# Layer 1 of a two-layer convolution and attention model: normalization as one factor a token, sent to all partitions by DMA

## The chip, the cores and the metric

The kernel runs on one core of a Trainium2 chip. A core has four engines that compute: TensorE (PE in the profile) multiplies matrices, with weight loads shown apart (PEld); VectorE (DVE), ScalarE (ACT) and GpSimd (POOL) work on elements. SyncE (SP) starts DMA transfers, one after the other, in the order of its own instructions. TensorE writes to PSUM, which has eight banks of 128 partitions by 512 fp32 values; DVE and ACT read it from there[...]. The metric is the time of one execution on the device in microseconds. Everything is fp32, but for two masks.

## The reference

The input x has the shape (4, 128, 64, 64). Layer 0 is a convolution and a local attention in windows of 16 by 16. Layer 1 takes each of the 4 x 4096 pixels as a token of 128 channels, and it normalizes every token twice: ahead of a linear causal attention, and ahead of a recurrent network.

```python
def _ln_t(v, eps=1e-5):
    m = jnp.mean(v, axis=-1, keepdims=True)
    s = jnp.var(v, axis=-1, keepdims=True)
    return (v - m) / jnp.sqrt(s + eps)

def _L1_attn_ref(x, W, b):
    qkv = (x @ W.T + b).reshape(Bx, Tx, 3, Dx)
    q, k, v = (qkv[:, :, 0], qkv[:, :, 1], qkv[:, :, 2])
    q = jax.nn.elu(q) + 1.0
    k = jax.nn.elu(k) + 1.0
    # num = q . cumsum(k v^T), den = q . cumsum(k)
    return num / den

def _L1_ffn_ref(x, W, V, gamma, beta):
    Wx = jnp.einsum('bti,hi->bth', x, W)
    # Wx normalized over all tokens (mean and variance of each channel), then
    # the recurrence yt = sigmoid(wx_t + yt @ V.T) over the tokens
    ...

x = _L0_conv_ref(x, ...)              # layer 0
t = _to_tokens(x)                     # layer 1
t = t + _L1_attn_ref(_ln_t(t), L1_attn_W, L1_attn_b)
t = t + _L1_ffn_ref(_ln_t(t), L1_ffn_W, L1_ffn_V, L1_ffn_gamma, L1_ffn_beta)
```

## The kernel before

The image is worked on in 16 bands of 16 rows (1024 tokens), each with four windows of layer 0. While TensorE goes through the windows of one band, layer 1 of the band before it is worked on in between: it is cut into small steps, and after each part of a window (six gaps a window) one step of layer 1 and one of the next band's convolution are put in. `in_order` then fixes that order on TensorE, DVE, ACT and GpSimd. SP's own order is left to the scheduler. A band of layer 1 has two halves of 512 tokens, `a` and `c`; `y` and `z` are the two halves of the band before, whose last steps are still due.

```python
p1, p2, p3 = ...   # pools with 1, 2 and 3 buffers a tag; bank() is one of 8 PSUM banks

def measured(pieces, eps):              # mean and 1/sqrt(var + eps) of each token
    for j, piece in enumerate(pieces):
        nc.vector.bn_stats(st[:, j, :], piece)                                # L191
    for j in range(n):
        nc.vector.bn_aggr(mv[:, j, :], st[:, j, :])                           # L193
    nc.gpsimd.tensor_scalar(rs[:, :n], mv[:, :n, 1], eps, 1.0, ALU.add, ALU.mult)  # L195
    nc.gpsimd.tensor_tensor(rs[:, :n], rs[:, :n], mhalf[:, :n], ALU.pow)      # L196
    return pieces, mv, rs

def normed(found, tiles, tag):          # tokens lie on partitions here
    for j, piece in enumerate(pieces):
        nc.vector.tensor_scalar(                                              # L203
            xn[:, j, :], piece, mv[:, j, 0:1], rs[:, j : j + 1], ALU.subtract, ALU.mult
        )
    return xn

def turned(xn, j0, n):                  # channels to partitions, through TensorE
    tps = bank()
    for j in range(n):
        nc.tensor.transpose(tps[:, j * P : (j + 1) * P], xn[:, j0 + j, :], ident)  # L212
    return tps

def taps(...): ...                      # convolution: eight multiply-adds of DVE, L288

def window_inputs(w, n, wj): ...        # q, k (L337), v (L350); two small DMAs for v (L359, L360)

def weighted(w):                        # layer 0: sums of the softmax, and its output
    ...                                 # sums on TensorE (L400)
    nc.scalar.copy(den, dps)                                                  # L403
    nc.sync.dma_start(dc, den[::HD, :])                                       # L405
    yield
    ...                                 # attention output on TensorE (L412)
    nc.scalar.copy(o_sb, ops)                                                 # L420
    yield
    nc.vector.tensor_tensor(dc, dc, pad_c, ALU.add)                           # L423
    nc.vector.reciprocal(rc, dc)                                              # L425
    nc.sync.dma_start(rd.rearrange("h (a e) -> (h a) e", e=16), rc)           # L429
    nc.sync.dma_start(rden, rd.unsqueeze(1).to_broadcast([HEADS, HD, BR * WT]))  # L431
    w["o"], w["rden"] = o_sb, rden

def scaled(n, wj, w):                   # output divided by the sums
    nc.gpsimd.tensor_tensor(oTs[n][...], w["o"]..., w["rden"]..., ALU.mult)   # L440

def output0(h):                         # layer 0's output, and x added
    ...
    nc.tensor.matmul(yps[:, j * P : (j + 1) * P], oT[:, br, t], woT[:, br, :], ...)  # L465
    nc.vector.tensor_tensor(h.x, yps..., xin[h.n][...], ALU.add)              # L472

def measure(h):
    h.found = measured([h.x[:, j, :] for j in range(4)], 1e-5)

def norm(h):
    h.xn = normed(h.found, p3, "xn")

def turn(h):
    h.xl = p2.tile([P, 512], F32, tag="xl", name="xl")
    nc.scalar.copy(h.xl, turned(h.xn, 0, 4))                                  # L489

def feature(h, m):                      # queries and keys: L494 on TensorE, L496 on ACT,
    ...                                 # L498 and L499 on DVE
def values(h): ...                      # L511 on TensorE, L519 on DVE
def scores(h): ...                      # L537 on TensorE, L539 on DVE
def attend(h, e): ...                   # L573, L575 on TensorE; L583 to L587 on DVE add to h.x

def keep(h):                            # x turned, for the very last addition
    rs = p1.tile([P, SEG, HSEGS], F32, tag="rs_o", name="rs_o")
    nc.scalar.copy(rs, turned(h.x, 0, 4).rearrange("p (k s) -> p s k", s=SEG))  # L592
    nc.sync.dma_start(resd[h.b][:, h.hb], rs.rearrange("p s k -> p (s k)"))   # L593

def turn_last(h):
    h.xl = p2.tile([P, 512], F32, tag="xl2", name="xl2")
    nc.scalar.copy(h.xl, turned(h.xn, 0, 4))                                  # L597

def product(h):                         # W x of the recurrent network, and its statistics
    wps = bank()
    nc.tensor.matmul(wps, fwT, h.xl, start=True, stop=True)                   # L602
    nc.scalar.copy(wx[:, h.b, h.hb], wps.rearrange("p (k s) -> p s k", s=SEG))  # L603
    nc.vector.bn_stats(stats[...], wx[...])                                   # L604
```

Behind the bands comes a short second phase: the kept x is loaded again from HBM (L748), and the recurrence runs in 128 segments side by side, eleven steps to warm up and then 32 (L771 to L823).

Of the kernel before, what the change touches and what calls it, by code (L numbers as in the profile page):

```python
# [9 lines left out]
F32 = mybir.dt.float32  # L10
# [36 lines left out]
def conv_attn_hybrid(ctx: ExitStack, tc: tile.TileContext, ins: dict, out: bass.AP):  # L47
# [10 lines left out]
    def loaded(name, shape, dt=F32, src=None, eng=None):  # L58
# [19 lines left out]
        pattern=[[1, P]],  # L78
        channel_multiplier=-1,
    )  # L80
    mhalf = const.tile([P, NCH], F32, name="mhalf")
    nc.vector.memset(mhalf, -0.5)

# [49 lines left out]
    def prepare():  # L133


        rect = math.sqrt(1.0 + LAM * LAM * (BR - 1))
        nc.vector.tensor_scalar(woT[:, 0], woT[:, 0], 1.0 / rect, None, ALU.mult)
        nc.vector.tensor_scalar(woT[:, 1], woT[:, 1], LAM / rect, None, ALU.mult)
        nc.vector.tensor_scalar(ab1, ab[:, :2], 1.0, None, ALU.add)


    dmax = const.tile([P, 16], F32, name="dmax")
# [33 lines left out]
    def bank():  # L176
        return ps.tile([P, 512], F32, tag="bank", name="bank")
# [21 lines left out]
    def normed(found, tiles, tag):  # L199
        pieces, mv, rs = found  # L200
        xn = tiles.tile([P, 4, P], F32, tag=tag, name=tag)
# [5 lines that stand above are left out]
# [272 lines left out]
            del oTs[h.n], xin[h.n]  # L479

    def measure(h):
        h.found = measured([h.x[:, j, :] for j in range(4)], 1e-5)

    def norm(h):
        h.xn = normed(h.found, p3, "xn")

    def turn(h):
        h.xl = p2.tile([P, 512], F32, tag="xl", name="xl")
        nc.scalar.copy(h.xl, turned(h.xn, 0, 4))  # L489

    def feature(h, m):

# [95 lines left out]

    def keep(h):

        rs = p1.tile([P, SEG, HSEGS], F32, tag="rs_o", name="rs_o")
        nc.scalar.copy(rs, turned(h.x, 0, 4).rearrange("p (k s) -> p s k", s=SEG))  # L592
        nc.sync.dma_start(resd[h.b][:, h.hb], rs.rearrange("p s k -> p (s k)"))  # L593

    def turn_last(h):
        h.xl = p2.tile([P, 512], F32, tag="xl2", name="xl2")
        nc.scalar.copy(h.xl, turned(h.xn, 0, 4))  # L597

    def product(h):

        wps = bank()
        nc.tensor.matmul(wps, fwT, h.xl, start=True, stop=True)  # L602
        nc.scalar.copy(wx[:, h.b, h.hb], wps.rearrange("p (k s) -> p s k", s=SEG))  # L603
        nc.vector.bn_stats(  # L604
            stats[:, h.b * NH + h.hb, :], wx[:, h.b, h.hb].rearrange("p s k -> p (s k)")
        )

    def layer1(n, last):
# [2 lines left out]
        y, z = last  # L611
        order = [
            (keep, z), None,
            (norm, z), (product, y), None,
            (output0, a), (measure, a), None,
            (turn_last, z), None,
            (norm, a), (output0, c), (measure, c), None,
            (turn, a), None,
            (product, z), (norm, c), None,
            (queries, a), None,  # L620
            (keys, a), None,
            (turn, c), None,
            (values, a), None,
            (queries, c), None,
            (scores, a), None,
# [5 lines left out]
            (attend, a, 0), None,  # L631
            (attend, a, 1), (measure, a), None,
            (scores, c), (keep, a), None,
            (accumulate, c), (norm, a), None,
            (attend, c, 0), None,
            (turn_last, a), (attend, c, 1), (measure, c), None,
        ]
        for what in order:
            if what is None:
# [5 lines left out]
    halves = {}  # L645

    def layer1_end(y, z):
        norm(z)
        product(y)
        yield  # L650
        keep(z)
        turn_last(z)
        yield
        product(z)

# [43 lines left out]
    for i in range(len(places) + 2):  # L699
# [5 lines left out]
        if 2 <= i:  # L705
            m, wjm = places[i - 2]
            if wjm == NB - 1:
                run(behind)
                behind = layer1(m, halves.pop(m - 1, (None, None)))
        between(i, 0)  # L710
        if 2 <= i:
            scaled(m, wjm, windows.pop(i - 2))
# [802 lines left out]
```

## Time and profile before

| | |
|---|---|
| time, median of 3 | 934.3 us (933.74 to 934.84) |
| span of the profiled run | 930.9 us |
| busy: PE, weight loads, DVE | 876.9, 656.1, 741.1 us |
| busy: ACT, POOL | 539.1, 262.4 us |
| granted TensorE clock | 0.975 |
| moved by DMA | 63.46 MB |

The page names each group of instructions by line, engine, operation and tiles. A timeline line has the start, the time taken, the engine, the line, the operation, and in brackets how long the engine had stood idle and what ended that. Several instructions of one line in a row are merged, with their count behind an x, and the time of such a group runs up to the end of its last one. Matmuls overlap, so what one of them costs is read from the next start, not from its own duration.

### The profile page before, as it was taken

Reading aid. Unit: us, or ns where it says so; the run is one execution under the profiler, and the core shown is the slowest. Engines: PE = TensorE matmul, PEld = TensorE weight load, DVE = VectorE, ACT = ScalarE, POOL = GpSimd, SP = SyncE. Lnnn points to the kernel's source line nnn. Section 1 sums busy time; section 2 is a strip of 40 time slices with the busy share of each in tenths; the row PEclk is TensorE's granted clock in tenths of the full one; section 3 lists DMA queues with packets and bytes.
Section 4 is the critical chain, followed back from the end, with each engine's and each line's share of the span. In section 5 each row is a group of like instructions: output and inputs, shape, how many; then the busy total and the mean of one; then the engine's idle time right before and its main releaser. Section 6 shows DMA issues by size and latency. Waiting matters only on the chain.

```text
span 930.9 us, 26534 instructions
## 1 busy us (share of the span) xinstructions
PE 876.9 (94%) x10508; PEld 656.1 (70%) x10508; DVE 741.1 (80%) x2452; ACT 539.1 (58%) x1010; POOL 262.4 (28%) x359
## 2 busy tenths in 40 slices
PE   4978999999999999999999999999999999987985
PEld 3756777877777777777787777787777777755442
DVE  6464978888897988797988888798878786676886
ACT  3755566565756565656656575656566665422552
POOL 2122131413232322313041323232232312121184
PEclk9988999999999999999999999999999999988897
DMA  4111121121222121212121121212121111102853
GB/s 121 34 44 56 47 72 37 54 57 57 59 63 59 49 57 50 69 49 73 37 56 57 52 59 60 62 48 62 48 66 48 49 37 60 43 24 73 345 205 129
DMA packets 53045, 63.46 MB, mean 68 GB/s; under 512 B 22960, under 2 KB 33840, under 8 KB 52400
## 3 DMA queue, kind: packets, MB, share of 16 engines
q1 hardware_dynamic: 51184, 56.91, 19.8%
q10 hardware_dynamic: 1728, 4.77, 1.3%
q8 instruction: 85, 1.39, 0.6%
q14 instruction: 48, 0.39, 0.1%
HBM read 35.44 MB, written 17.30 MB: 57 GB/s over the span
## 4 chain that ended last, share of the span: by engine, by line
PE 60%; DVE 26%; issue 4%; ACT 4%; DMA 3%; POOL 3%; ACTq 0%; SPq 0%; DVEq 0%; POOLq 0%
DVE y L288 8%; PE bank L337 8%; PE bank L465 6%; PE bank L382 6%; PE bank L212 6%; PE bank L494 5%; PE bank L400 4%; PE bank L350 4%; PE bank L412 4%; PE bank L602 3%; DVE st L191 2%; PE bank L815 2%; PE bank L537 2%; PE bank L573 2%; DVE state L562 2%
## 5 line engine op out<-in xcount | busy, mean ns | idle before, releaser
L288 DVE SCALAR_TENSOR_TENSOR y<-ypad,cpe_w,y 128x512 f32<-128x512 f32 x240 | 189.8, 791 | 15.1 <-ACT y L286 11.7
L391 ACT ACTIVATE es<-bank 128x512 f32<-128x512 f32 x256 | 132.2, 603 | 77.1 <-PE bank L382 77.1
L440 POOL TENSOR_TENSOR oT<-o_sb,rden 128x512 f32<-128x512 f32 x64 | 86.6, 1354 | 243.1 <-DMA rden<-rd 165.8
L195 POOL TENSOR_SCALAR rs<-mv 128x4 f32<-128x4 f32 (+2 forms) x100 | 25.1, 251 | 364.4 <-DVE mv L193 163.2
L203 DVE TENSOR_SCALAR xn<-x,mv,rs 128x128 f32<-128x128 f32 x256 | 90.8, 416 | 26.5 <-POOL rs L196 26.5
L196 POOL TENSOR_TENSOR rs<-rs,mhalf 128x4 f32<-128x4 f32 (+2 forms) x100 | 106.2, 1062 | 8.3
L382 PEld LDWEIGHTS bank<-q,k 32*128 32x128 f32 x3072 | 97.7, 189 | 7.8 <-ACT k L345 6.6
L382 PE MATMUL bank<-q,k 32*128 32x96 f32 (+1 forms) x3072 | 96.3, 270 | 1.1 <-ACT k L345 1.1
L412 PEld LDWEIGHTS bank<-es,v_sb 128*32 128x32 f32 x3072 | 56.8, 110 | 30.2 <-issue 18.6
L465 PE MATMUL bank<-woT,oT 128*128 128x128 f32 x512 | 68.1, 289 | 5.7 <-POOL oT L440 5.7
L465 PEld LDWEIGHTS bank<-woT,oT 128*128 128x128 f32 x512 | 64.8, 202 | 9.7 <-POOL oT L440 7.3
L412 PE MATMUL bank<-es,v_sb 128*32 128x96 f32 (+1 forms) x3072 | 70.1, 240 | 0.0
L494 PE MATMUL bank<-xl,awT 128*128 128x512 f32 x128 | 70.0, 630 | 0.0
L400 PE MATMUL bank<-es,ones 128*32 128x512 f32 x512 | 69.1, 612 | 0.0
L357 ACT COPY v_sb<-bank 128x512 f32<-128x512 f32 x64 | 37.5, 586 | 53.5 <-PE bank L350 42.2
L337 PE MATMUL bank<-y2w,wqT 128*128 128x256 f32 x256 | 66.4, 382 | 1.0 <-DVE y2w L288 1.0
L337 PE MATMUL bank<-y2w,wkT 128*128 128x256 f32 x256 | 65.8, 380 | 0.0
L350 PE MATMUL bank<-wvT,y2w 128*128 128x256 f32 x256 | 65.8, 380 | 0.0
L345 ACT COPY q<-bank 128x512 f32<-128x512 f32 x64 | 37.6, 587 | 41.3 <-PE bank L337 39.2
L345 ACT COPY k<-bank 128x512 f32<-128x512 f32 x64 | 37.3, 583 | 36.8 <-PE bank L337 36.7
L191 DVE BATCH_NORM_STATS2 st<-x 128x6 f32<-128x128 f32 x256 | 55.5, 280 | 1.1
L337 PEld LDWEIGHTS bank<-y2w,wqT 128*128 128x128 f32 x256 | 45.8, 194 | 12.8 <-issue 7.2
(124 smaller groups left out, 1728.4 us busy)
## 6 DMA issues: line engine op xcount, KB each, us to landing
rden<-rd SPq DMA_DIRECT2D x64, 256.0 KB
v_sb<-v_sb SPq DMA_DIRECT2D x128, 64.0 KB
resd<-rs_o SPq DMA_DIRECT2D x32, 256.0 KB
out<-ot SPq DMA_DIRECT2D x32, 256.0 KB
xin<-in_xt SPq DMA_DIRECT2D x15, 512.0 KB
res<-resd SPq DMA_DIRECT2D x2, 2048.0 KB
res<-resd ACTq DMA_DIRECT2D x2, 2048.0 KB
dc<-den SPq DMA_DIRECT2D x64, 8.0 KB
```

What stands on the lines that cost most here:

```text
L196: nc.gpsimd.tensor_tensor(rs[:, :n], rs[:, :n], mhalf[:, :n], ALU.pow)
L203: nc.vector.tensor_scalar(xn[:, j, :], piece, mv[:, j, 0:1], rs[:, j : j + 1], ALU.subtract, ALU.mult)
L288: nc.vector.scalar_tensor_tensor(y2, src, cpe_w[:, tap : tap + 1], y2, ALU.mult, ALU.add)
L337: nc.tensor.matmul(pps[:, br * WT : (br + 1) * WT], wT[:, br * P : (br + 1) * P], y2, start=True, stop=True,)
L350: nc.tensor.matmul(vps[:, e * 256 : (e + 1) * 256], y2[:, e * P : (e + 1) * P], wvT, start=True, stop=True,)
L382: nc.tensor.matmul(sps[h][:, cols], w["k"][rows, k0 : k0 + P], w["q"][rows, cols], start=False, stop=(br, n) == pieces[-1],)
L391: nc.scalar.activation(es, sps[h], AF.Exp, scale=scale)
L400: nc.tensor.matmul(dps[rows], ones[:, :HD], w["es", h], start=True, stop=True)
L412: nc.tensor.matmul(ops[rows, cols], w["v"][:, n, c0 : c0 + HD], w["es", h][:, cols], start=(br, n) == pieces[0], stop=(br, n) == pieces[-1],)
L440: nc.gpsimd.tensor_tensor(oTs[n][:, :, :, wj * WS : (wj + 1) * WS], w["o"].rearrange("p (a r c) -> p a r c", a=BR, c=WS), w["rden"].rearra ...
L465: nc.tensor.matmul(yps[:, j * P : (j + 1) * P], oT[:, br, t], woT[:, br, :], start=br == 0, stop=br == BR - 1,)
L494: nc.tensor.matmul(zps, awT[:, m * P : (m + 1) * P], h.xl, start=True, stop=True)
```

## The change

The normalization of layer 1 is (x - mean) times one factor a token. Both parts are taken out of the elementwise work on x. The mean is removed by the weights: with C = I - 1/128, W C x is W (x - mean), so awT and fwT are multiplied by C once. The factor rs stays as a multiplication of whole tokens, and it may come behind the transposes, or behind W, where tokens lie along the free axis. For that, rs is needed on all partitions: it is written to HBM (2 KB) and read back by every partition (256 KB). The second transposition of x, `turn_last`, goes away with its copy: `keep` has x turned already, and `product` now takes it from there. The order of the steps is changed so that the factor has some gaps to arrive in. What ACT copied out of PSUM in `turn` and `product` is now multiplied by DVE.

```diff
+    center = const.tile([P, P], F32, name="center")
+    nc.vector.tensor_scalar(center, ident, -1.0 / P, None, ALU.add)
...
+    def centre(w):
+        cps = bank()[:, : w.shape[1]]
+        nc.tensor.matmul(cps, center, w, start=True, stop=True)
+        nc.vector.tensor_copy(w, cps)
...
     def measure(h):
-        h.found = measured([h.x[:, j, :] for j in range(4)], 1e-5)
-
-    def norm(h):
-        h.xn = normed(h.found, p3, "xn")
+        _, _, rs = measured([h.x[:, j, :] for j in range(4)], 1e-5)
+        there = dram4.tile([P, 4], F32, tag="rs_d", name="rs_d")
+        nc.sync.dma_start(there, rs)
+        h.rs = p3.tile([P, 512], F32, tag="rs_b", name="rs_b")
+        nc.sync.dma_start(h.rs, there.rearrange("p j -> (p j)").partition_broadcast(P))

     def turn(h):
         h.xl = p2.tile([P, 512], F32, tag="xl", name="xl")
-        nc.scalar.copy(h.xl, turned(h.xn, 0, 4))
+        nc.vector.tensor_tensor(
+            h.xl.rearrange("p (j t) -> p j t", j=4),
+            turned(h.x, 0, 4).rearrange("p (j t) -> p j t", j=4),
+            h.rs.rearrange("p (t j) -> p j t", j=4),
+            ALU.mult,
+        )
...
     def keep(h):
-        rs = p1.tile([P, SEG, HSEGS], F32, tag="rs_o", name="rs_o")
-        nc.scalar.copy(rs, turned(h.x, 0, 4).rearrange("p (k s) -> p s k", s=SEG))
-        nc.sync.dma_start(resd[h.b][:, h.hb], rs.rearrange("p s k -> p (s k)"))
-
-    def turn_last(h):
-        h.xl = p2.tile([P, 512], F32, tag="xl2", name="xl2")
-        nc.scalar.copy(h.xl, turned(h.xn, 0, 4))
+        h.xs = p2.tile([P, SEG, HSEGS], F32, tag="rs_o", name="rs_o")
+        nc.scalar.copy(h.xs, turned(h.x, 0, 4).rearrange("p (k s) -> p s k", s=SEG))
+        nc.sync.dma_start(resd[h.b][:, h.hb], h.xs.rearrange("p s k -> p (s k)"))

     def product(h):
         wps = bank()
-        nc.tensor.matmul(wps, fwT, h.xl, start=True, stop=True)
-        nc.scalar.copy(wx[:, h.b, h.hb], wps.rearrange("p (k s) -> p s k", s=SEG))
+        nc.tensor.matmul(wps, fwT, h.xs.rearrange("p s k -> p (s k)"), start=True, stop=True)
+        n = P // SEG
+        nc.vector.tensor_tensor(
+            wx[:, h.b, h.hb].rearrange("p s (j n) -> p s j n", n=n),
+            wps.rearrange("p (s j n) -> p s j n", n=n, j=4),
+            h.rs.rearrange("p (n s j) -> p s j n", n=n, j=4),
+            ALU.mult,
+        )
...
         order = [
             (keep, z), None,
-            (norm, z), (product, y), None,
+            (product, y), None,
             (output0, a), (measure, a), None,
-            (turn_last, z), None,
-            (norm, a), (output0, c), (measure, c), None,
-            (turn, a), None,
-            (product, z), (norm, c), None,
-            (queries, a), None,
+            (output0, c), (measure, c), None,
+            None,
+            (product, z), None,
+            (turn, a), None,
+            None,
+            (queries, a), (turn, c), None,
             (keys, a), None,
-            (turn, c), None,
             (values, a), None,
...
             (attend, a, 1), (measure, a), None,
             (scores, c), (keep, a), None,
-            (accumulate, c), (norm, a), None,
+            (accumulate, c), None,
             (attend, c, 0), None,
-            (turn_last, a), (attend, c, 1), (measure, c), None,
+            (attend, c, 1), (measure, c), None,
...
     def layer1_end(y, z):
-        norm(z)
         product(y)
         yield
         keep(z)
-        turn_last(z)
         yield
         product(z)
...
+        if i == 2:
+            centre(awT)
+            centre(fwT)
```

## The prediction, made before the changed kernel ran

> **What bounds the kernel now.** I read the busy shares first, then the table by stage, the chain that ended last, TensorE's timeline over one band, and last the waits. The stage table (columns: stretch, its length, then busy us of PE, weight loads, DVE, ACT, POOL, each with its count, the granted clock, DMA share and GB/s) says that from 126 to 779 us TensorE is never short of work:
>
> ```profile
> 277.00:327.00 50.00, 49.57 (x649) 37.83 (x641) 42.48 (x142) 31.02 (x58) 14.01 (x19) 1.00 0.20 55
> 429.00:479.00 50.00, 49.76 (x629) 37.93 (x632) 43.00 (x143) 30.91 (x58) 14.19 (x19) 1.00 0.19 56
> 821.00:862.00 41.00, 31.78 (x168) 23.31 (x168) 29.14 (x102) 11.81 (x20) 5.76 (x13) 0.83 0.14 51
> ```
>
> In the middle TensorE has 49.6 of 50 us, DVE 42.5 and ACT 31; in the last band (821 to 862) nobody is full, so latency counts there. Matmul ends are modelled, so I checked on the timeline whether the starts really follow each other. They do, with few holes. Around the meeting of two bands:
>
> ```profile
> 420.93 1.01 PE L212 MATMUL bank<-ident,xn 128*128 128x128 f32 x4
> 421.77 0.39 PE L573 MATMUL bank<-v,aT 128*128 128x129 f32 x2
> ...
> 427.91 1.09 PE L412 MATMUL bank<-es,v_sb 128*32 128x96 f32 x48
> 428.93 2.05 PE L465 MATMUL bank<-woT,oT 128*128 128x128 f32 x16
> 430.82 1.03 PE L337 MATMUL bank<-y2w,wqT 128*128 128x256 f32 x4
> 431.69 0.60 PE L212 MATMUL bank<-ident,xn 128*128 128x128 f32 x4
> 432.12 1.03 PE L337 MATMUL bank<-y2w,wkT 128*128 128x256 f32 x4
> ```
>
> Four transposes at 431.69 push the next matmul back by 0.43 us: 0.109 each, that is their real price, not the 0.27 of the group's mean. The four at 420.93 took 0.84 until the next start, because each waited for one normalization on DVE. The same bands repeat at L465 starts of 378.39, 428.93, 479.39, 529.49: 50.4 us a band.
>
> What can hold L465 besides TensorE is oT, the product that GpSimd forms once rden, the softmax divisors, have come back by DMA. It is nearly as late as TensorE already:
>
> ```profile
> 417.96 0.19 POOL L195 TENSOR_SCALAR rs<-mv 128x4 f32<-128x4 f32 x1
> 418.24 1.01 POOL L196 TENSOR_TENSOR rs<-rs,mhalf 128x4 f32<-128x4 f32 x1
> ...
> 426.80 1.28 POOL L440 TENSOR_TENSOR oT<-o_sb,rden 128x512 f32<-128x512 f32 x1
> ```
> ```profile
> 417.17 0.32 SPq L593 DMA_DIRECT2D resd<-rs_o  x1
> 419.20 0.33 SPq L429 DMA_DIRECT2D rd<-rc  x1
> 420.66 0.58 SPq L431 DMA_DIRECT2D rden<-rd  x1
> ```
>
> oT ends at 428.08 and L465 starts at 428.93: slack 0.85 us. By the trace's record of landings rd takes 1.40 us and rden 5.34, so rden is there at 426.00, 0.80 before oT starts. In some bands (378.39, 580.22) L465 starts only when oT ends.
>
> **What the Trainium skill says.** (1) "DMA: Bandwidth & Descriptors", section "Why a DMA increments its semaphore by 16 and not by 1": a transfer is spread over as many engines as divide its outermost dimension. The trace agrees: rden (outermost 4, 256 KB) takes a median 5.25 us, resd (128 rows, 256 KB) 2.00. The new broadcast has 128 outermost, so I take 2.0 us for it when nothing is ahead. (2) "SBUF — State Buffer", section "SBUF: two separate sides": DVE and GpSimd exclude each other on a shared port for a whole instruction. The trace agrees: L203 mostly takes 0.34 us, but up to 1.31 beside GpSimd. Removing L203 removes these. (3) "SBUF — State Buffer", section "Door 1: The DMA port swizzle": each access that leaves a 16-byte line costs extra. The new multiply reads rs_b in steps of 16 bytes; no operation here shows the size of it.
>
> **The change part by part.** *Removed.* TensorE: 4 transposes for each of 32 halves (turn_last), 128 x 0.109 = 14.0 us, plus the waits for xn at 420.93, some 0.4 us a band. DVE: 256 normalizations, 90.8 us busy. ACT: the copies L489, L597 and L603, 19.0 + 18.8 + 20.1 = 57.9 us. *Added.* DVE: two multiplies a half from PSUM, 64 x 0.685 (as L519 and L472 of the same shape) = 43.8 us, perhaps 1.0 each with the strided operand. DMA: 64 writes of 2 KB and 64 broadcasts of 256 KB, 16.8 MB on top of 63.5, all in the one SP queue. Two centring matmuls once, with their copies to SBUF: about 0.5 us of it seen. DVE falls by 47 and ACT by 58 us; neither is the bound, so this is worth little by itself.
>
> If only TensorE counted, a band would lose 8 x 0.109 + 0.4 = 1.3 us, and 15 bands 19 us: 915. But the order of the instructions on SP says otherwise. In the last window of a band it becomes: write of rs, resd, rd, broadcast of rs, rden. In time of the old trace: rs leaves GpSimd at 419.25, its write is issued at 419.3, resd at 419.65 and rd at 420.0 instead of 419.20. Now resd stands right ahead of rd; where this happens already (812.4 and 812.8) rd took 1.79 instead of 1.40. It lands at 421.8, rden is issued at 421.9 instead of 420.66, and lands at about 427.4. oT then runs until 428.7 and L465 starts at 428.8, not 428.93, though TensorE would be there at 428.0. Of the gain ahead of L465 only 0.15 us is left. The transposes at 431.69 are behind L465, and their 0.44 is gained in full. So 0.6 us a band, 14 full bands: -8.4.
>
> *Turn and product.* From rs(a) ready (434.3) I count 1.5 for the write, then xin's 512 KB stands ahead (landing at 438.6 or so), then the broadcast: 439.3. DVE is ready for turn(a) at 438.4 and stands 0.9 us, while the queries' matmul comes at 441: hidden. For c the write waits behind rden's engines until about 442.6, and its broadcast lands at about 445; DVE stands 1.5 us for turn(c). Before, DVE idled 1.2 us at 452, and that is what pays for it: hidden, but only just.
>
> *Last band.* The late rden costs 1.8 us, less the 0.4 gained: +1.4. There the way from statistics to the first projection becomes 1.4 + 2.0 + 0.7 in place of normalization, transposes and copy (1.1 + 0.4 + 0.6): +2.0, of which shorter DVE queues give back 1.5. The end of layer 1 has the same trade and no large balance. +0.5.
>
> Sum: 934.3 - 8.4 + 1.4 + 0.5 + 0.5 = 928.3, put at 928.
>
> **The rivals.** *A, TensorE alone bounds it.* If rden comes as early as before (resd and rd not in each other's way), the 1.3 us a band are gained in full: 914 to 917. For it: PE is 60% of the chain, and DVE and ACT are relieved. Against it: 0.80 us of slack ahead of oT and at least 0.8 of added issue time in the same queue. *B, the broadcasts come late.* If turn(c)'s factor lands 1 us later than I count, or the strided multiply takes 1.1 us, DVE goes late into its full stretch (403 to 420 in the trace has no idle time), rc and rden slip with it, and each band pays 0.6 to 1.5 us: 937 to 950. For it: transfers issued behind xin and rden in this trace take 4.5 to 5.9 us instead of 1.9. Against it: the features of a, the next thing on DVE, come ahead of turn(c). *C, nothing to be seen.* oT takes up all of it, 932 to 935.
>
> **Range and chances.** My own account gives 928, A the lower edge (914), B beyond the upper (943). A at its best barely reaches the 2% line (915.6), so faster by over 2% gets 0.12. Slower by over 2% needs more than 953, B at its worst and in every band: 0.08. The rest, 0.80, lies within.
>
> **What would show it.** Right, if in the changed profile the bands repeat every 49.6 to 50.0 us, L465 waits for oT in most bands (the list of waits gives 5 of its matmuls and 5 of its weight loads now, 13.0 us in all; then 20 or more), rden is issued 1.0 to 1.5 us later after the attention sums than before, and DVE waits about 1 us for rs_b in each turn. Wrong towards A, if L465 has no more waits for oT and bands take 49.1. Wrong towards B, if TensorE waits for xl ahead of the queries, or the multiply has a mean above 1 us. Wrong altogether, if the last band and the recurrence behind it move by more than 4 us.

## The result, and the profile after

The changed kernel takes 1046.6 us (median of four runs) against 934.6 for the kernel before beside it: 1.120 times as long, with a 95% interval of 1.116 to 1.124. The prediction was 928, within 914 to 943. It is wrong by 119 us.

Where do they lie? In the two profiled runs (1044.3 and 930.9 us) I take the start of output0's first matmul in each band (L474 now, L465 before) as a mark. From the first band's mark to the last band's it is 839.3 us now and was 745.1: +94. From the last mark to the first matmul of the warm-up behind layer 1 (L822 now, L803 before) it is 63.0 and was 41.2: +22. Everything else is 2.6 us shorter. The middle bands repeat every 56.5 us instead of 50.3.

First the table by stage of the changed kernel, one band and the end of layer 1, with the columns of the prediction:

```profile
529.00:585.00 56.00, 50.56 (x636) 39.09 (x637) 41.42 (x129) 27.91 (x50) 13.28 (x19) 0.97 0.28 69
915.00:978.00 63.00, 29.10 (x156) 22.31 (x156) 28.53 (x87) 7.24 (x12) 5.81 (x13) 0.69 0.45 163
```

TensorE is busy 50.6 of 56 us, so it no longer sets the pitch, and the granted clock has left 1.00. The timeline where two bands meet shows what happens there (line numbers have moved by 9: L449 is oT, L474 output0, L346 q):

```profile
526.97 0.59 ACT L429 COPY o_sb<-bank 128x512 f32<-128x512 f32 x1
527.73 1.26 POOL L449 TENSOR_TENSOR oT<-o_sb,rden 128x512 f32<-128x512 f32 x1 [3.03 <-DMA rden<-rd]
...
529.04 2.64 PE L474 MATMUL bank<-woT,oT 128*128 128x128 f32 x16 [2.19 <-POOL oT L449]
...
531.48 1.91 PE L346 MATMUL bank<-y2w,wqT 128*128 128x256 f32 x4
```

TensorE stands for 2.19 us, because oT stands for rden. The matmul L346, which took 1.03 us at the same place before, then takes 1.91. The table by stage, cut at the change of the clock, says why (only the granted clock, the third number from the right, matters here):

```profile
529.00:530.30 1.30, 1.26 (x11) 1.26 (x12) 0.00 (x0) 0.00 (x0) 0.00 (x0) 1.00 0.38 107
530.30:533.70 3.40, 3.40 (x15) 3.04 (x14) 1.91 (x11) 0.27 (x1) 0.01 (x1) 0.50 0.35 116
```

A pause of 2.2 us is followed here by 3.4 us at half the clock, which costs 1.7 us more. Before, the clock records show half clock for 0.8 us between the first and last marks, the first 15 us left out; now for 64.0 us.

Not every such pause is followed by half clock. In this trace the half-clock records begin and end on one grid of 3.41 us, and what counts is how much of one interval of this grid TensorE stands. The pause shown lies with 2.13 us inside the interval from 526.92 to 530.33, and the next interval is at half clock. A longer pause, from 245.57 to 248.41, is split by the grid into 1.46 and 1.39 us, and the clock stays. Of the 223 intervals between the marks that begin at full clock, 15 are followed by half clock; in these TensorE stands for 2.03 to 2.55 us, but for one with 1.56. In the other 208 it stands for at most 1.89.

Why is rden late? SyncE's queue ahead of this pause:

```profile
518.15 0.32 SPq L494 DMA_DIRECT2D rs_d<-rs  x1
518.57 0.57 SPq L609 DMA_DIRECT2D resd<-rs_o  x1
519.24 0.38 SPq L438 DMA_DIRECT2D rd<-rc  x1
519.89 0.32 SPq L496 DMA_DIRECT2D rs_b<-rs_d  x1
522.12 0.58 SPq L440 DMA_DIRECT2D rden<-rd  x1
```

The order is the one predicted: rs_d, resd, rd, rs_b, rden. By the trace's record of landings, in us from issue to landing:

```
               this band   median of all   before
resd             3.32          3.69          2.00
rd               2.83          1.45          1.40   (p75: 2.92 now, 1.42 before)
rs_b             4.04          3.91           -     (3.08 the fastest, 17.56 the slowest)
rden             5.47          5.35          5.25
```

rd (8 KB) lands at 522.06, and only then can rden be issued. In this band the broadcast rs_b goes out behind rd; resd, ahead of rd, and rd itself are slow all the same. The waits of all bands together:

```profile
PE bank L474 <- POOL oT L449: 49.7, 16, 8.1
PEld bank L474 <- POOL oT L449: 53.8, 16, 8.9
PE bank L510 <- DVE xl L500: 38.7, 20, 8.1
DVE xl L500 <- DMA rs_b<-rs_d: 55.0, 25, 4.8
DVE wx L616 <- DMA rs_b<-rs_d: 22.6, 3, 17.0
PE bank L391 <- ACT k L354: 8.0, 4, 2.4
```

All 16 bands stand for oT now (5 before, 7.3 us by the weight loads). A second stop is new: TensorE stands for xl ahead of the queries, and xl for the broadcast. A third, for k (the last line), is smaller; e2 below shows where it comes from.

At the end of layer 1 the last broadcast is caught behind the loads of the result:

```profile
954.19 0.32 SPq L767 DMA_DIRECT2D res<-resd  x1
954.56 0.43 SPq L496 DMA_DIRECT2D rs_b<-rs_d  x1
```
```profile
972.14 1.02 DVE L616 TENSOR_TENSOR wx<-bank,rs_b 128x512 f32<-128x512 f32 x1 [16.98 <-DMA rs_b<-rs_d]
```
```profile
973.22 1.46 PE L808 MATMUL bank<-zeros 128*128 128x256 bf16 x6 [21.16 <-DVE wx L616]
```

The loads move 8 MB in four transfers; a broadcast that starts beside them lands after 17.56 us instead of 3.9. That is some 14 of the +22.

Last, the chain, which was 60% PE before:

```profile
DVE 34%; DMA 31%; PE 22%; POOL 5%; issue 4%; ACT 3%; SPq 0%; ACTq 0%; DVEq 0%; POOLq 0%
```

### The profile page after: what moved, and what is told of

Its sections match the earlier page's. It is cut to its first block, busy times and chain, and to the rows that moved or that the text cites. A ratio compares the mean times of both kernels' runs of the same rounds, so it can differ in the third digit from the quotient of the medians.

```text
span 1044.3 us, 26158 instructions
## 1 busy us (share of the span) xinstructions
PE 879.3 (84%) x10384; PEld 666.8 (64%) x10384; DVE 731.4 (70%) x2263; ACT 489.7 (47%) x914; POOL 252.3 (24%) x359
## 4 chain that ended last, share of the span: by engine, by line
DVE 34%; DMA 31%; PE 22%; POOL 5%; issue 4%; ACT 3%; SPq 0%; ACTq 0%; DVEq 0%; POOLq 0%
DVE y L297 11%; DMA rden<-rd 8%; DMA rs_d<-rs 8%; DMA rs_b<-rs_d 7%; PE bank L474 7%; DMA rd<-rc 6%; DVE st L200 4%; PE bank L346 3%; DVE state L578 3%; DVE f L515 3%; POOL oT L449 2%; POOL rs L205 2%; DVE x L603 2%; DVE low L514 2%; PE bank L510 2%
## 5 line engine op out<-in xcount | busy, mean ns | idle before, releaser
L297 DVE SCALAR_TENSOR_TENSOR y<-ypad,cpe_w,y 128x512 f32<-128x512 f32 x240 | 182.5, 761 | 24.9 <-ACT y L295 21.0
L449 POOL TENSOR_TENSOR oT<-o_sb,rden 128x512 f32<-128x512 f32 x64 | 83.5, 1304 | 367.1 <-DMA rden<-rd 239.2
L474 PE MATMUL bank<-woT,oT 128*128 128x128 f32 x512 | 81.2, 326 | 49.7 <-POOL oT L449 49.7
L474 PEld LDWEIGHTS bank<-woT,oT 128*128 128x128 f32 x512 | 77.9, 237 | 55.2 <-POOL oT L449 53.8
L510 PE MATMUL bank<-xl,awT 128*128 128x512 f32 x128 | 73.0, 653 | 40.6 <-DVE xl L500 38.7
L205 POOL TENSOR_TENSOR rs<-rs,mhalf 128x4 f32<-128x4 f32 (+2 forms) x100 | 99.0, 990 | 8.3
L481 DVE TENSOR_TENSOR x<-bank,xin 128x512 f32<-128x512 f32 x32 | 22.1, 692 | 102.6 <-PE bank L474 102.6
L512 ACT ACTIVATE low<-bank,ab 128x512 f32<-128x512 f32 x64 | 44.0, 688 | 83.2 <-PE bank L510 83.2
L346 PE MATMUL bank<-y2w,wqT 128*128 128x256 f32 x256 | 75.3, 422 | 1.0 <-DVE y2w L297 1.0
L500 DVE TENSOR_TENSOR xl<-bank,rs_b 128x512 f32<-128x512 f32 x32 | 34.1, 1067 | 59.7 <-DMA rs_b<-rs_d 55.0
L346 PE MATMUL bank<-y2w,wkT 128*128 128x256 f32 x256 | 65.8, 379 | 0.0
L514 DVE TENSOR_SCALAR low<-low 128x512 f32<-128x512 f32 x64 | 40.7, 635 | 33.4 <-ACT low L512 33.4
L616 DVE TENSOR_TENSOR wx<-bank,rs_b 128x512 f32<-128x512 f32 x32 | 33.9, 1060 | 41.6 <-DMA rs_b<-rs_d 22.6
```

What stands on the lines that cost most here:

```text
L297: nc.vector.scalar_tensor_tensor(y2, src, cpe_w[:, tap : tap + 1], y2, ALU.mult, ALU.add)
L346: nc.tensor.matmul(pps[:, br * WT : (br + 1) * WT], wT[:, br * P : (br + 1) * P], y2, start=True, stop=True,)
L449: nc.gpsimd.tensor_tensor(oTs[n][:, :, :, wj * WS : (wj + 1) * WS], w["o"].rearrange("p (a r c) -> p a r c", a=BR, c=WS), w["rden"].rearra ...
L510: nc.tensor.matmul(zps, awT[:, m * P : (m + 1) * P], h.xl, start=True, stop=True)
L514: nc.vector.tensor_scalar(low, low, 1.0, None, ALU.min)
```

## The experiments

My first theory: the transfers are the whole loss, and the arithmetic of the change is worth what it promised. The loss comes (a) from what they do to rd, rden and dc behind them in the queue, (b) from waits for the factor itself, (c) from the end, (d) from the clock. A rival: the strided multiply (1.07 us instead of the estimated 0.685) makes DVE late.

### The transfers alone, and the arithmetic alone

The kernel before with the transfers, their result unused (e1):

```diff
     def measure(h):
         h.found = measured(...)
+        there = dram4.tile([P, 4], F32, tag="rs_d", name="rs_d")
+        nc.sync.dma_start(there, h.found[2])
+        unused = p1.tile([P, 512], F32, tag="rs_b", name="rs_b")
+        nc.sync.dma_start(unused, there.rearrange("p j -> (p j)").partition_broadcast(P))
```

> The kernel before, with the 64 writes of rs and the 64 broadcasts added and nothing reading them (one buffer for the broadcast). Queue theory (the new transfers stand ahead of rd and rden in the one queue, rden is late, oT is late, L465 waits, and the pause costs clock on top): bands of 51.7 to 53.5 us instead of 50.4, 955 to 985 us in all. Multiply theory (the transfers are harmless by themselves; what costs is DVE's wait for the factor and its slow strided multiply): at most 940 us, bands of 50.4 to 50.7.

Measured: 991.1 us, ratio 1.062 (1.059 to 1.065). Bands of 53.8 us; the end of layer 1 (41.7) nearly as before (41.2). The broadcast has a median of 3.92 us, resd 3.62.

```profile
PEld bank L465 <- POOL oT L440: 34.7, 16, 6.4
DVE dc L423 <- DMA dc<-den: 37.5, 24, 3.3
```

Transfers that nobody reads cost 57 us. So (a) is real. In e1 it reaches dc as well as rden (waits for dc before: 7.5 us); in the changed kernel dc is waited for no longer than before (6.2 us).

The changed kernel without them (e2). A tile of ones stands for the factor, read in the same strides, so the scaling of layer 1's norms is left out:

```diff
-        there = dram4.tile([P, 4], F32, tag="rs_d", name="rs_d")
-        nc.sync.dma_start(there, rs)
-        h.rs = p3.tile([P, 512], F32, tag="rs_b", name="rs_b")
-        nc.sync.dma_start(h.rs, ...)
+        h.rs = factor
```

> The changed kernel without the writes and broadcasts: the factor is a constant tile of ones, read in the same strided way (so layer 1 is not normalized by its variance). Queue theory: all waits go, only TensorE counts: bands of 49.1 us, 912 to 920 us. Multiply theory: the strided multiply of 1.06 us in place of 0.69 stays, DVE stays late and bands stay above 51 us: 945 us or more.

Measured: 917.9 us, ratio 0.982 (0.979 to 0.986), with the multiply still at 1.11 us. So the multiply is not the cause, and the transfers cost 1046.6 - 917.9 = 128.7 us in this kernel. Three bands, one an image, took 52 to 54 us, the others mostly 48 to 49. The timeline of such a band, GpSimd and ACT:

```profile
182.14 0.19 POOL L206 TENSOR_SCALAR rs<-mv 128x4 f32<-128x4 f32 x1 [1.47 <-DVE mv L204]
182.41 1.01 POOL L207 TENSOR_TENSOR rs<-rs,mhalf 128x4 f32<-128x4 f32 x1
...
183.38 0.21 POOL L281 COPY ypad<-ypad 128x17 f32<-128x17 f32 x1
...
184.07 0.81 ACT L297 ACTIVATE y<-ypad,cpe_b,cpe_w 128x512 f32<-128x512 f32 x1 [5.10 <-POOL ypad L285]
...
184.79 0.56 ACT L356 COPY k<-bank 128x512 f32<-128x512 f32 x1
...
185.41 1.40 PE L393 MATMUL bank<-q,k 32*128 32x96 f32 x20 [2.35 <-ACT k L356]
```

The change measures the third product one gap earlier. GpSimd then computes its factor ahead of the padding copies, ACT stands 5.1 us for these, k waits behind it on ACT, and TensorE waits for k. To test it, output0 and the measuring went back to their gap (e7, still with ones for factors):

```diff
-            (output0, c), (measure, c), None,
             None,
+            (output0, c), (measure, c), None,
```

> The changed kernel without its transfers (factors of one from a fixed tile), with output0 and the measuring of the third product put back to the gap they had in the kernel before. If the move set GpSimd's factors ahead of the padding copies and that costs the 5 us once an image: the long bands of 52 to 54 us go to 48 to 49, time 900 to 908 us. If the long bands come from something else: time 915 to 920 us as without this edit.

Measured: 909.8 us, 0.976 (0.973 to 0.979). The long bands are gone, the mean is 48.9, and between the marks (the first 15 us again left out) the clock is never halved. The padding copies now come at 180.98.

### The end, and the clock

The loads of the result held back until the last product is done, by one copied column of wx (e3):

```diff
+    nc.vector.tensor_copy(res[:, :, 0, 0, 0], wx[:, :, NH - 1, SEG - 1, HSEGS - 1])
     for b in range(B):
         (nc.sync, nc.scalar)[b % 2].dma_start(res[:, b]..., resd[b])
```

> The changed kernel, with the four loads of the kept x held back until the last product is done (one copy of four elements a partition into res ahead of them). If the 17 us wait at the end comes from the last broadcast standing behind those loads, it lands in 3 to 4 us instead of 17.6, and the time falls by 11 to 15 us, to 1032 to 1036. If it is the broadcast itself that is slow there, nothing changes.

Measured: 1039.6 us, 1.113 (1.109 to 1.117). The end of layer 1 goes from 63.0 to 48.4 us, but the later loads give 6.6 us back behind it (72.7 instead of 66.1). So the collision with the loads costs 15 us, and half of what its undoing gains is lost again. Of the +22 some 7 remain: TensorE still waits 7.4 us for wx there.

Nine bf16 matmuls that fill TensorE's pause ahead of each band's first L474 (e4):

```diff
+        if h.s == 0:
+            fill = bank()
+            for _ in range(9):
+                nc.tensor.matmul(fill, zeros, zeros[:, :1].to_broadcast([P, 512]), ...)
```

> The changed kernel with nine idle bf16 matmuls (0.21 us each) ahead of each band's first L474, into the pause where TensorE waits for oT (2.2 us). Clock theory (the pause is followed by 3.4 us at half clock, 1.7 us lost a band): the granted clock stays at 1.0 in the bands, a band falls from 56.3 to 54.6 us, 20 to 26 us in all: 1020 to 1027. If the half clock costs nothing because oT and xl set the pace anyway: 1044 to 1050, though the clock rises.

Measured: 1033.2 us, 1.109 (1.104 to 1.113). Half clock between the marks fell from 64.0 to 30.3 us, worth 17 us where TensorE is busy throughout; 13.4 were gained. The half clock follows the pauses and is a cost of its own, if less than I had expected.

### What makes the broadcast slow and its neighbours late

e1 with 128 different rows of 2 KB read instead of one row 128 times: the same bytes, and the queue still waits for the small write (e5; 61.5 us in all, 117.4 in e1):

```diff
-        nc.sync.dma_start(there, h.found[2])
-        nc.sync.dma_start(unused, there.rearrange("p j -> (p j)").partition_broadcast(P))
+        nc.sync.dma_start(there[:, :4], h.found[2])      # there: one of four tiles of 128 x 2 KB
+        nc.sync.dma_start(unused, there)
```

> The kernel before with the 64 unused factor transfers of the first run, but what is sent to all partitions is 128 different rows of 2 KB in HBM (256 KB, four tiles filled once) instead of one row of 2 KB read 128 times; it still stands behind the same small write. If the many reads of one small place make the broadcast slow (3.9 us) and its neighbours with it (resd 3.6 us): broadcast about 2.0 us, resd 2.0 to 2.5 us, time under 975 us. If it is the number of bytes and the place in the queue alone: both as in the first run, time 985 to 995 us.

Measured: 939.7 us, 1.009 (1.006 to 1.013). The read has a median of 2.72 us (fastest 2.52), resd 2.53.

```profile
PEld bank L465 <- POOL oT L440: 12.7, 11, 5.2
DVE dc L423 <- DMA dc<-den: 9.0, 6, 3.1
```

Of 57 us 6 are left, at the same number of bytes. But this edit had also spread the small write: its 16-byte pieces no longer lie side by side. So that was undone alone (e8):

```diff
-        nc.sync.dma_start(there[:, :4], h.found[2])
+        nc.sync.dma_start(there[0].rearrange("(p j) -> p j", j=4), h.found[2])
```

> As the run before it with 128 different rows, but the factors are written as in the changed kernel: 128 pieces of 16 bytes side by side in one row of 2 KB, the first of the 128 rows that are then read. If the 128 reads of one row are what is slow: broadcast 2.5 to 2.8 us, resd about 2.5 us, time 936 to 946 us. If it is the writing of small pieces next to each other, which the run with different rows had also taken away: broadcast over 3.3 us, time 980 to 995 us.

Measured: 965.8 us, 1.036 (1.031 to 1.040): neither number. The read has a median of 3.27 us (fastest 2.42), and the small write 2.21 instead of 1.41; the queue waits 91.4 us in all for it. Of e1's 57 us the form of the write holds about 26 (965.8 - 939.7) and the form of the read about 25 (991.1 - 965.8).

The row copied to 16 rows first, each then read 8 times (e9):

```diff
+        copies = dram4.tile([16, 512], F32, tag="rs_c", name="rs_c")
+        nc.sync.dma_start(copies, there.rearrange("p j -> (p j)").partition_broadcast(16))
+        nc.sync.dma_start(unused, copies.unsqueeze(1).to_broadcast([16, P // 16, 512]))
```

> The kernel before with 64 unused factor transfers, where the row is first copied to 16 rows in HBM, and each of the 16 is then read 8 times. If many reads of one place are the cost: the broadcast lands in 2.5 to 2.9 us, and the time is 938 to 955 us although a third wait stands in the queue. If reading what has just been written, or waits in the queue, are the cost: 985 to 1010 us.

Measured: 992.5 us, 1.062 (1.058 to 1.066), no better than one row, though with a third transfer to each factor. The read itself may gain: in v3 below it takes 3.28 us from 16 copies (median; 2.97 at its fastest), in v4 4.07 from one row (3.10), but the two also differ in when they issue it. What in e5's pattern makes it cheap is not settled.

Was it the wait between write and broadcast, which stops all later issues of SyncE? e10 let each broadcast read the row of one measuring earlier:

```diff
+        earlier.append(there)
+        if len(earlier) > 2:
+            earlier.pop(0)
-        nc.sync.dma_start(unused, there...)
+        nc.sync.dma_start(unused, earlier[0]...)
```

> The kernel before with the same 64 small writes and 64 unused broadcasts of one row of 2 KB, but each broadcast reads the row written one measuring earlier, which has landed long ago, so the queue holds no wait between the two. If the wait of the queue for the small write is what delays rden and dc behind it: 936 to 955 us, the waits for oT and dc near those of the kernel before. If the reads of one row are the cost: 975 to 992 us, as with the wait.

Measured: 985.2 us, 1.055 (1.051 to 1.059). It decides nothing: the order of issue is chosen by a scheduler, which moved the broadcast up to the write that it reads, and the queue still waited 109 us for small writes (117 in e1). e13 holds it in place by a small GpSimd copy into its tile (0.19 us each), and reads the row of two measurings earlier:

```diff
+        nc.gpsimd.tensor_copy(unused[:, :1], h.found[2][:, :1])
         earlier.append(there)
-        if len(earlier) > 2:
+        if len(earlier) > 3:
```

> The kernel before with the 64 small writes and 64 unused broadcasts, each broadcast of the row written two measurings earlier, and kept in its place behind the new small write by one GpSimd copy of a column; the queue now has no wait for the small write. (In the run before with an earlier row, the broadcasts had been scheduled up to the write that they read, so that the wait stayed.) If the queue's wait of some 110 us in all for the small write is what delays rden and dc: 938 to 958 us. If the reads themselves are the cost: 975 to 992 us.

Measured: 1018.8 us, 1.093 (1.089 to 1.097): slower than with the wait. The waits of TensorE's weight loads, and of the queue:

```profile
PEld bank L465 <- POOL oT L440: 65.0, 16, 9.6
```
```profile
SPq L431 <- DMA rd<-rc: 123.8, 48, 5.9
```
```profile
566.22 0.32 SPq L486 DMA_DIRECT2D rs_d<-rs  x1
566.59 0.42 SPq L492 DMA_DIRECT2D rs_b<-rs_d  x1
567.11 0.38 SPq L603 DMA_DIRECT2D resd<-rs_o  x1
567.54 0.42 SPq L429 DMA_DIRECT2D rd<-rc  x1
572.50 0.57 SPq L431 DMA_DIRECT2D rden<-rd  x1
```

The queue's wait for the small write is gone. Now broadcast and resd go out back to back ahead of rd, and rd's 8 KB land after 4.95 us instead of 1.4; rden is issued then. (The added copies make GpSimd itself stand 8.7 us in all for earlier broadcasts, too little for the 28 us between e13 and e1.) So the wait as such is not the whole cost: with it or without, slow transfers of 256 KB around rd delay rd or its issue. The Trainium skill, "DMA: Bandwidth & Descriptors", section "Queues, rings and completion order", says that each engine takes the pieces of one queue in their order; rd's 4.95 us behind two large transfers agree.

### rden in another form

rden (outermost dimension 4) as four transfers of 32 partitions, in the changed kernel (e6) and in the kernel before (e11):

```diff
-        nc.sync.dma_start(rden, rd.unsqueeze(1).to_broadcast([HEADS, HD, BR * WT]))
+        for h in range(HEADS):
+            nc.sync.dma_start(rden[h * HD : (h + 1) * HD, :], rd[h].partition_broadcast(HD))
```

> The changed kernel with rden sent as four transfers of 32 partitions each, one a head, instead of one transfer whose outermost dimension is 4. If rden's own length (5.4 us, few of the 16 DMA engines at work) is what turns a late rden into the pause ahead of the band's first matmul: rden lands in 2.5 to 3.5 us, the pause of 2.2 us and the half clock behind it go in most bands, time 1000 to 1020 us. If the queue ahead of rden is what holds it: rden lands no earlier, time 1040 to 1050 us.

> The kernel before with rden alone sent as four transfers of 32 partitions, no factor transfers. If rden's 5.3 us were on the path of the kernel before: up to 10 us less, 922 to 930 us. If TensorE alone sets the pitch of its bands, as the prediction read it: 931 to 936 us. It also says how much of the 63 us that this edit gave the changed kernel was the undoing of a new delay.

Measured: e6 983.2 us, 1.054 (1.048 to 1.061), with 2.86 us for each part of rden (median); e11 926.3 us, 0.994 (0.992 to 0.996). The waits of e6:

```profile
PEld bank L475 <- POOL oT L450: 20.2, 15, 6.0
PE bank L511 <- DVE xl L501: 35.4, 13, 7.3
```

63 us are gained in the changed kernel and 6 before (932.6 to 926.3; by the ratio, 4 to 7), so some 57 of the 63 undo a delay that the change brought. The wait for xl stays. e11 is the fastest version that has all of the computation; the gain is small.

The factors sent by GpSimd, which makes them (e12):

```diff
-        nc.sync.dma_start(there, rs)
+        nc.gpsimd.dma_start(there, rs)
...
-        nc.sync.dma_start(h.rs, ...)
+        nc.gpsimd.dma_start(h.rs, ...)
```

> The changed kernel with its two factor transfers issued by GpSimd, which makes the factors, instead of by the queue of SyncE; nothing else moved. If the wait in SyncE's queue was the main cost: rden and dc come no later than in the kernel before and most of the bands recover, time 950 to 990 us. If GpSimd now stands for the small write instead, and delays oT with it: 1020 to 1060 us.

Measured: 1117.6 us, 1.196 (1.192 to 1.201), beyond both ranges.

```profile
POOL rs_b L496 <- DMA rs_d<-rs: 158.0, 59, 5.1
```

GpSimd stands for the small write, with oT and the padding copies behind it. rden gets no shorter (median 5.42 us), but three quarters of the rd now land within 1.43 us (2.92 in the changed kernel). The skill's page just named, section "Issuing engines are not separate DMA queues", says that the transfers of all issuers meet on the same 16 engines; no run here shows whether rd is quick because of the other issuer or because the broadcasts now come at other times.

### Can a part of the change be kept?

Four versions have the last band's second norm as in the kernel before. In v1 only the second norm's factor is sent, one or two gaps later, GpSimd's part of it included:

```diff
+            (send, y), (send, z), (turn, c), None,
+            (spread, y), (values, a), None,
+            (spread, z), (queries, c), None,
...
+            (multiplied, y), (values, c), None,
```

> A version that keeps the kernel before in the first norm, and takes the second norm's factor by transfer behind W, but asks for it one to two gaps later than the changed kernel and multiplies still later, so that no engine waits for it; the last band of all is as before, so that nothing stands behind the loads of the result. 32 broadcasts instead of 64, none close ahead of rden. If lateness in the queue alone was the cost: bands shorter by 0.9 to 1.4 us (two groups of turning matmuls gone), time 912 to 925 us. If any broadcast in the queue costs whatever its place, as in the first run: about half of that run's added 57 us, time 950 to 965 us.

Measured: 1026.0 us, 1.099 (1.096 to 1.103).

```profile
SPq L618 <- POOL rs L615: 100.6, 12, 17.5
```

Lateness had been moved to a worse place: GpSimd computed the factor behind oT, SyncE waited for it up to 17.5 us, and dc and v stood behind (TensorE waits 53.7 us in all for v). v3 computes it right behind the measuring and spreads three transfers over three gaps (16 copies, rden in four); v4 is the same without copies:

```
v3          (scores, c), (keep, a), (send, skip), None,
            (accumulate, c), ..., (copy16, skip), None,
            (attend, c, 0), (spread, skip), None,
v4          (scores, c), (keep, a), (send, skip), None,
            (accumulate, c), ..., None,
            (attend, c, 0), (spread, skip), None,
```

> The second norm alone as a factor by transfer, from 16 copies, with each of its three transfers issued one gap after the other so that none stands in the queue for long, GpSimd's part of it right behind the measuring, and rden as four transfers. If reads of one place and waits in the queue were the whole cost: two groups of turning matmuls less a band are kept as gain, time 912 to 925 us. If any further broadcast costs by its bytes alone: 940 to 960 us.

> The second norm alone by transfer as in the run that came to 932 us, without the copying to 16 rows; the small write one gap behind the measuring, the broadcast two gaps behind the write, and the multiplication later again, so that the queue never waits for the write. If waits in the queue are all that was left of the cost: 914 to 925 us. If two more transfers a band cost by being there: 928 to 936 us.

Measured: v3 932.1 us, 0.997 (0.995 to 0.999); v4 933.9 us, 1.001 (0.999 to 1.004). Both have rden's new form too, and with that alone (e11, 0.994) it is 926. So two broadcasts a band, well placed, still cost more than the saved matmuls bring: by the ratios some 3 us in v3 and 7 in v4. v2 does the same with both norms, each transfer one gap behind the other:

```diff
+            (send, a), None,
+            (copy16, a), (output0, c), (measure, c), (pick, c), None,
+            (multiplied, y), (spread, a), (send, c), None,
+            (copy16, c), (multiplied, z), None,
+            (turn, a), (spread, c), None,
```

> Both norms of the changed kernel as factors by transfer, from 16 copies, each transfer one gap behind the other, the two turnings one to two gaps later, the order of the padding copies as in the kernel before, rden as four transfers, and the last band's second norm as in the kernel before. If the causes found are all there are: the time of the changed kernel without transfers (910 us) plus some 5 us, 905 to 922 us. If four broadcasts a band still crowd the queue so that turning waits for them: 940 to 980 us.

Measured: 1047.4 us, 1.123 (1.119 to 1.127).

```profile
PE bank L511 <- DVE xl L501: 101.5, 16, 9.1
```

The first norm has no time for this: queries wait for xl, and every gap given to the queue is taken from TensorE.

Last, the changed kernel with three causes undone together: rden in four, the old gap for the third product, the last band's second norm on the chip (e14):

```diff
+        for h in range(HEADS): ...                       # rden, as in e6
-            (output0, c), (measure, c), None,
             None,
+            (output0, c), (measure, c), None,
+        second = measure_last if ends else measure       # last band as before
```

> The changed kernel with three things undone: rden in four transfers, the place of output0 and of measuring the third product as before, and the last band's second norm on the chip as before; all other 62 broadcasts stay. If the causes add: 983 less 8 for the order less 20 for the end, 950 to 962 us. If the once-an-image 5 us is hidden behind the other waits: 960 to 968 us.

Measured: 961.1 us, 1.028 (1.022 to 1.033). 85 of 112 us are back, 6 short of the sum (955), so how far the causes add is not quite settled. What is left are the waits of TensorE for the factor (L511) and, above the 5.7 us before, for oT (L475), less what the arithmetic saves:

```profile
PE bank L511 <- DVE xl L501: 38.7, 19, 7.4
PE bank L475 <- POOL oT L450: 17.2, 13, 4.6
```

## Why the prediction was wrong, point by point

**What bounds the kernel: right for the middle bands.** TensorE set the pitch and oT was nearly as late: in e11 an earlier rden moves the middle bands before from 50.3 only to 50.2. The time of e11, 926.3, fell into the range given for an rden on the path (922 to 930), and it is there at both ends: of the 6.6 us between the profiled spans 3.1 lie ahead of the second mark and 1.8 behind the last.

**What the arithmetic brings: right.** The text had 1.3 us a band and 915 us "if only TensorE counted"; e7, which leaves out only the sending of factors and keeps the old gap, has 1.4 us a band and 909.8. The multiply took 1.07 us, not 0.685 (the text allowed for "perhaps 1.0"), but DVE had room for it. The move of the third product cost 8 us by way of GpSimd's order; it was nowhere in the sum. (8 us is e2 less e7; in the changed kernel TensorE stands 7.1 us between the marks for this k.)

**The failed step: "I take 2.0 us for it when nothing is ahead", and with it "so 0.6 us a band".** The 2.0 came from resd, a write of 128 rows to HBM. The read of one row by 128 partitions took 3.08 us at its fastest and 3.91 in the median; that 128 rows are spread over all engines was right and said nothing of such a read. The larger part of the error is what the broadcast does to its neighbours, those just ahead of it included. The text let resd delay rd to 1.79 us and the broadcast cost rden one issue slot. In the changed kernel resd goes out within 1.5 us ahead of rd 15 times, and rd took 2.74 to 4.53 us there; in e2, without the transfers, it did so twice, with 1.76 and 2.00. In the band shown: rd 2.83 us, rden issued 1.4 us later than in the account of the same order (522.12 against 421.9 + 98.85 = 520.75, where 98.85 us lie between rs_d's issue here, 518.15, and there, 419.3). The account had TensorE stand for 0.8 us there (428.0 to 428.8). The direction was right, but it stood for 2.2.

**"Hidden, but only just": failed.** The text had the factor of turn(a) land 5.0 us after it was computed (434.3 to 439.3), with xin's 512 KB ahead of it landing at 438.6. In the band shown it took 7.9 (534.97 to 542.89):

```profile
536.16 0.33 SPq L109 DMA_DIRECT2D xin<-in_xt  x1
536.64 0.33 SPq L496 DMA_DIRECT2D rs_b<-rs_d  x1
542.98 1.05 DVE L500 TENSOR_TENSOR xl<-bank,rs_b 128x512 f32<-128x512 f32 x1 [2.53 <-DMA rs_b<-rs_d]
544.08 1.12 PE L510 MATMUL bank<-xl,awT 128*128 128x512 f32 x2 [1.99 <-DVE xl L500]
```

The order was right, and the broadcast landed 0.85 us behind xin, 0.7 in the text. What was mis-sized is xin: it landed 7.1 us after the factor was computed (542.04), not 4.3. The trace before could have told: there xin took 6.15 us from its issue, landing at 442.26:

```profile
436.11 0.33 SPq L106 DMA_DIRECT2D xin<-in_xt  x1
```

TensorE stands for xl 20 times, 38.7 us in all.

**What was missing: the clock.** No step asked what TensorE does after a stop. The skill, "TensorE: Matmul & The Clock Gate", section "What's actually happening", gives half rate after an idle window of about 3.4 us; here 2.2 us of standing still were enough where they fell into one interval of the grid, and the half rate held for 3.4 us or a multiple of it, which fits the page's window. The 63 us more of half clock cost about 30 us: TensorE is busy for 744.9 us between the marks, and for 714.5 in e7, which has neither the transfers nor these stops.

**Last band and end: "+0.5", measured +22.** That the last broadcast is issued right behind the loads of the result was nowhere in the prediction. The late rden of the last band was there with +1.4; TensorE stands 8.1 us for oT at the last mark (2.5 before).

The account of the +94 between the marks, from the gaps of TensorE's timeline: it stands for 86.9 us more (42.6 for oT, 30.6 for xl, 7.1 for the k of e2, 4.8 for x in the transposes of L221, 1.8 for the rest) and is busy for 7.4 us more (23.0 less by the arithmetic, as in e7, and 30.4 more at half clock).

**The rivals.** B had the right name (broadcasts late, TensorE waiting for xl, multiply above 1 us) and a size four to ten times too small, since it counted one late factor and not the transfers behind it. The sign given for "wrong altogether" (last band and recurrence off by over 4 us) and both signs of B have come; of the signs for "right" only the waits of L474 in most bands did.

**Shown and not shown.** Shown: the transfers cost 129 us (e2) and 57 even unused (e1); about 57 by what rden's form cures (e6 with e11), some 15 at the end, of which half came back as it was undone (e3), 8 through GpSimd's order (e7, without transfers). Not shown: why reading 128 different rows is cheap while copying the row to 16 first gains nothing, and how a broadcast slows resd and rd that were issued just ahead of it. Rows all freshly written but different were not tried.

## What to carry to other kernels

A transfer that replaces arithmetic is paid for by the transfers around it in the same queue: ask for each small one (here rd, 8 KB) whose result gates an engine what now stands close ahead of it and close behind, and take the new one's duration from a transfer of the same direction and pattern. Where an engine has under 1 us of slack, a delay becomes a stop, and a stop of TensorE can bring half clock on top. Before building such a change, put its transfers, unused, into the kernel before: e1 alone would have shown the first 57 us.

## What the runs showed of the hardware

- 256 KB from one row of 2 KB in HBM to 128 partitions: 3.08 us at its fastest in the changed kernel, 3.9 in the median; from 128 different rows 2.52 and 2.72 (e5; 2.42 and 3.27 in e8); the write of 128 rows (resd, before) 2.00.
- That write took 3.69 us in the median beside such broadcasts, and 1.99 in the same kernel without them (e2).
- A multiply by an operand in steps of 16 bytes (xl) or more (wx), 128x512: 1.06 to 1.11 us on DVE instead of 0.685.
- TensorE in the changed kernel: half clock for 3.41 us or a multiple, on one fixed grid; an interval with 2.03 us or more of standing was followed by it, one with up to 1.89 was not, but for one with 1.56.
- A broadcast beside 8 MB of loads: 17.56 us.
